# A graph network in one kernel: the second layernorm's shift made by GpSimd, and three older arrangements of layernorm work put in place of newer ones

## The chip, the cores and the metric

The kernel runs on one core of one Trainium2 chip. The metric is device time in microseconds (us) of the whole program, median of 3 runs. Engines are named as in the profile: PE is TensorE (matmuls), PEld its weight loads, DVE is VectorE, ACT is ScalarE, POOL is GpSimd, SP is SyncE (it issues transfers here). "L85" is line 85 of the kernel before.

## The reference

Four graph layers, each with a residual and a layernorm. N is 4096 nodes, D is 256 features; `adj` is a 0/1 matrix of 4096 x 4096.

```python
def _layernorm(x, axis=-1, eps=1e-5):
    m = jnp.mean(x, axis=axis, keepdims=True)
    v = jnp.var(x, axis=axis, keepdims=True)
    return (x - m) / jnp.sqrt(v + eps)

# layer 0: graph attention, 8 heads of 32 features
node_feats = (x @ W.T + b).reshape(num_nodes, num_heads, half)
attn_logits = logit_parent[:, None, :] + logit_child[None, :, :]
attn_logits = jax.nn.leaky_relu(attn_logits, 0.2)
attn_logits = jnp.where(jnp.abs(adj_matrix)[..., None] != 0.0, attn_logits, 0.0)
attn_probs = jax.nn.softmax(attn_logits, axis=1)
out = jnp.einsum('ijh,jhc->ihc', attn_probs, node_feats)
# layer 1
A = DIAG_LAMBDA * jnp.diagonal(adj) + adj
out = A @ (x @ weight) + bias
# layer 2: two steps of diffusion (R) and of attention that keeps the top 0.9 of each row (A)
for n in range(STEPS):
    A = _top_p_attention(Xa, W1, W2, W3)
    Xf = R @ Xf
    Xa = A @ Xa
    Z = Z + Xf @ U1[n].T + Xa @ U2[n].T
h = X + Z          # then a layernorm of its own with gain and offset
# layer 3
agg = adj @ x / jnp.maximum(deg, 1.0)
out = jax.nn.relu(jnp.concatenate([x, agg], axis=-1) @ W + b)
# after each layer: x = _layernorm(x + layer(x))
```

In layer 1, `jnp.diagonal(adj)` is added to every row of `adj`; so every row of the product gets the same row vector, the sum of `diag[j] * support[j]`. The kernel calls it `row` once the bias is in it.

## The kernel before

Rows are held in 32 blocks (`NB`) of 128 partitions. `X` is the state, in SBUF throughout. A layernorm takes mean and variance on VectorE, the reciprocal deviation on GpSimd (L84, L85) and the normalise (L92) on VectorE or another engine:

```python
    def moments(self, pool, src):
        ...
        for q in range(n):
            nc.vector.bn_stats(stats[:, q, :], src[:, q, :])                                   # L81
            nc.vector.bn_aggr(mv[:, q, :], stats[:, q, :])                                     # L82
        nc.gpsimd.tensor_scalar_add(var, mv[:, :, 1], EPS)                                     # L84
        nc.gpsimd.tensor_tensor(rstd, var, self.power.to_broadcast([P, n]), ALU.pow)           # L85
        return mv, rstd

    def layernorm(self, pool, dst, src, engine=None):
        mv, rstd = self.moments(pool, src)
        for q in range(src.shape[1]):
            (engine or self.nc.vector).tensor_scalar(dst[:, q, :], src[:, q, :], mv[:, q, 0:1], rstd[:, q:q + 1],
                                                     op0=ALU.subtract, op1=ALU.mult)           # L92
```

Layer 0 works through two halves (heads 0 to 3, 4 to 7), four tiles `it` of 1024 rows each, four heads each: 32 heads' turns in all. In a head's turn, for each of 8 pieces, ScalarE or VectorE makes signs (L272, L265), VectorE makes the mask `gt` of them and of the adjacency (L274, L267), and PE multiplies it (L280):

```python
            self.sums0(both, nlc, fac, lpd, nad, zd, gmd, lambda: row_logits(first, 0, 0))
            self.open_x()
            self.load1()                        # issues layer 1's weight and bias, ScalarE's queue (L111, L117)
            ...
            later = []
            per_head = Q // 2 // (H // 2)       # 1
            for half in range(2):
                for it in range(N // IT):
                    ...
                    if half:
                        ...  # X rows and y0 (what the first half stored) are loaded
                    for hh in range(H // 2):
                        h = half * (H // 2) + hh
                        lpb = row_logits(work.tile([P, IT], F32, name="lpb"), h, it) if h or it else first
                        ...
                        for g in range(NB // K):
                            gt = work.tile([P, K, IT], FP8, name="gt", bufs=4)
                            ...  # signs (L265 or L272, four each), mask (L267 or L274), 32 matmuls (L280)
                        ...  # the head's tail on VectorE, L285 to L296: y
                        for xs in later[:per_head]:
                            self.layernorm(work, xs, xs, nc.gpsimd)
                        del later[:per_head]
                    if not half:
                        ...  # y is stored
                        continue
                    engine = nc.vector if i0 + Q == NB else nc.gpsimd
                    for q in range(0, Q, 2):
                        xs = X[:, i0 + q:i0 + q + 2, :]
                        engine.tensor_add(xs[:, :, :D // 2], xs[:, :, :D // 2], y0[:, q:q + 2])     # L308
                        engine.tensor_add(xs[:, :, D // 2:], xs[:, :, D // 2:], y[:, q:q + 2])      # L309
                        if i0 + Q == NB:
                            self.layernorm(work, xs, xs)
                        else:
                            later.append(xs)
```

At its very start (`sums0`) VectorE folds the attention vectors into the weights; `self.diag` is the diagonal, loaded during that part:

```python
            for t, cs in ((w0, (0, 1)), (b0, (0,))):
                for c in cs:
                    for s in range(2):
                        prod = work.tile([P, H, C], F32, name="prod", bufs=1)
                        nc.vector.tensor_mul(prod, ...)                                             # L390
                        nc.vector.tensor_reduce(t[:, c, D + s * H:D + (s + 1) * H], prod, AX.X, ALU.add)  # L391
            ...
            nc.vector.tensor_copy(self.diagr, self.diag)                                            # L456
```

Layer 1. The adjacency pieces of a block are made one block ahead, on VectorE (L185) and ScalarE (L183) in turn, and there is room for the pieces of two blocks:

```python
            row = pool.tile([P, D], F32, name="row1")
            nc.vector.tensor_add(row, pd[:, :D], bias)
            nc.vector.tensor_add(row, row, pd[:, D:])                                               # L699
            nas = []
            ahead = self.adj_pieces(work, nas, 0)
            for b in range(NB):
                ps = psum.tile([P, 512], F32, name="ps_adj")
                now, ahead = ahead, None
                for g, a in enumerate(now):
                    nc.sync.dma_start(self.adjs[b, :, g * 8:(g + 1) * 8, :], a.bitcast(F32))        # L708
                    for k in range(8):
                        jc = g * 8 + k
                        nc.tensor.matmul(ps, a[:, k, :], XD[:, jc]..., start=(jc == 0), stop=(jc == NB - 1))  # L711
                if b + 1 < NB:
                    ahead = self.adj_pieces(work, nas, b + 1)
                xb = X[:, b:b + 1, :]
                nc.vector.tensor_add(xb[:, 0], xb[:, 0], ps[:, :D])                                 # L716
                nc.vector.tensor_add(xb[:, 0], xb[:, 0], ps[:, D:])                                 # L717
                nc.vector.tensor_add(xb[:, 0], xb[:, 0], row)                                       # L718
                self.layernorm(work, xb, xb)
```

After a block is normalised, ScalarE issues its store `xd <- X` (L807, written in layer 2). Layer 2's second step ("step 1") closes each of the 32 blocks with two layernorms in a row; the second is applied by ScalarE (`fma`, the profile's L910) as `rstd * h + shift`:

```python
                    mv, rstd = self.moments(work, h)
                    shift = small("shift")
                    nc.vector.scalar_tensor_tensor(shift, mv[:, 0, 0:1], -1.0, rstd, op0=ALU.mult, op1=ALU.mult)  # L1290
                    fma(hb, hb, rstd, shift)
```

Of the kernel before, what the change touches and what calls it, by code (L numbers as in the profile page):

```python
# [9 lines left out]
F32 = mybir.dt.float32  # L10
I32 = mybir.dt.int32
F32R = mybir.dt.float32r
# [10 lines left out]
P = 128  # L23
# [28 lines left out]
class Net:  # L52
# [9 lines left out]
    def constants(self):  # L62
        nc = self.nc
        pool = self.ctx.enter_context(self.tc.tile_pool(name="const", bufs=1))
        self.ident = pool.tile([P, P], F32, name="ident")
        make_identity(nc, self.ident)
        self.power = pool.tile([P, 1], F32, name="power")
        nc.vector.memset(self.power, -0.5)
        self.deg = pool.tile([P, self.NB], F32, name="deg")
        self.diag = pool.tile([P, self.NB], F32, name="diag")  # L70
        self.diagr = pool.tile([P, self.NB], F32R, name="diagr")

# [14 lines left out]

    def layernorm(self, pool, dst, src, engine=None):

        mv, rstd = self.moments(pool, src)  # L90
        for q in range(src.shape[1]):
            (engine or self.nc.vector).tensor_scalar(dst[:, q, :], src[:, q, :], mv[:, q, 0:1], rstd[:, q:q + 1],  # L92
                                                     op0=ALU.subtract, op1=ALU.mult)

# [99 lines left out]
    def layer0(self):  # L194
# [7 lines left out]
        with ExitStack() as ctx:  # L202
# [9 lines left out]

            def row_logits(t, h, it):
                nc.gpsimd.dma_start(t, bass.AP(tensor=lpd.tensor, offset=lpd.offset + h * N + it * IT, ap=[[0, P], [1, IT]]))
                return t

            first = pool.tile([P, IT], F32, name="lpb0")


# [14 lines left out]
            na = gp.tile([P, NB, IT], U8, name="na")  # L234

            later = []
            per_head = Q // 2 // (H // 2)
            for half in range(2):
                for it in range(N // IT):
# [10 lines left out]
                    for hh in range(H // 2):  # L250
                        h = half * (H // 2) + hh
                        lpb = row_logits(work.tile([P, IT], F32, name="lpb"), h, it) if h or it else first
                        z = work.tile([P, Q, C1], F32, name="z")
# [42 lines left out]
                        nc.vector.tensor_mul(y[:, :, hh, :], t1[:, :, :C], r.unsqueeze(2).to_broadcast([P, Q, C]))  # L296
# [7 lines left out]

                    engine = nc.vector if i0 + Q == NB else nc.gpsimd
                    for q in range(0, Q, 2):
                        xs = X[:, i0 + q:i0 + q + 2, :]
                        engine.tensor_add(xs[:, :, :D // 2], xs[:, :, :D // 2], y0[:, q:q + 2])  # L308
                        engine.tensor_add(xs[:, :, D // 2:], xs[:, :, D // 2:], y[:, q:q + 2])  # L309
# [52 lines left out]

    def sums0(self, both, nlc, fac, lpd, nad, zd, gmd, then):

# [5 lines left out]
        with ExitStack() as ctx:  # L370
# [73 lines left out]
            self.factors0(wp, ps, both, nlc, fac)  # L444
            then()

# [231 lines left out]
    def layer1(self):  # L678
        nc, tc, NB, D, X = self.nc, self.tc, self.NB, self.D, self.X
        with self.ctx1 as ctx:  # L680
            pool, w1, bias, dg = self.pool1, self.weight1, self.bias1, self.diagr
            work = ctx.enter_context(tc.tile_pool(name="l1w", bufs=2))
# [20 lines left out]
            for b in range(NB):  # L703
# [14 lines left out]
                nc.vector.tensor_add(xb[:, 0], xb[:, 0], row)  # L718
                self.layernorm(work, xb, xb)


    def layer2(self):
# [3 lines left out]
        with ExitStack() as ctx:  # L726
# [543 lines left out]
            def close(step, b, two):  # L1270
# [12 lines left out]
                else:  # L1283
# [5 lines left out]
                    shift = small("shift")  # L1289
                    nc.vector.scalar_tensor_tensor(shift, mv[:, 0, 0:1], -1.0, rstd, op0=ALU.mult, op1=ALU.mult)  # L1290
                    fma(hb, hb, rstd, shift)
# [195 lines left out]
```

## Time and profile before

| | |
|---|---|
| time, median of 3 runs | 4482.35 us (4478.71 to 4483.64) |
| span of the profiled execution | 4477.0 us |
| PE busy | 4236.7 us, 95% |
| VectorE busy | 3339.2 us, 75% |
| ScalarE busy | 2759.6 us, 62% |
| GpSimd busy | 387.2 us, 9% |

A "group" in the profile is all instructions of one line, engine and shape: its count, its busy time in us, the mean of one in ns, and the idle time of the engine just before them with what ended it. The "chain of waits" lists who waited for whom, in total us, times, and the longest. Busy time is an average over stages with different limits. Layer 0's heads run from about 616 to 1350 us in this execution, layer 1 to 1637, layer 2's second step from about 2970 to 4215, layer 3 from there.

### The profile page before, as it was taken

The numbers are of one execution on the slowest core, as the hardware profiler recorded it, in microseconds if no ns is written. First come the engines' busy times: TensorE is split into PE (matmuls) and PEld (weight loads), VectorE is DVE, ScalarE is ACT, GpSimd is POOL, SyncE is SP. The second block draws the span as 40 slices with busy tenths as digits, with TensorE's granted clock in tenths as the row PEclk, the third lists the DMA queues.
The fourth block names the chain that finished last, engine by engine and source line by source line (L and its number), as shares of the span: only waits on it lengthen the run. The fifth ranks groups of instructions, "written<-read, shape, count | busy, mean of one in ns | idle before, by whom it ended". The sixth has DMA issues, their size and how long they took to land. (4 is left out here: it accounts for less than half of the span.)

```text
span 4477.0 us, 70563 instructions
## 1 busy us (share of the span) xinstructions
PE 4236.7 (95%) x25625; PEld 3409.6 (76%) x25625; DVE 3339.2 (75%) x7641; ACT 2759.6 (62%) x5501; POOL 387.2 (9%) x554
## 2 busy tenths in 40 slices
PE   8999989999989999999999999887999999999799
PEld 6899989999987866677777777664666666666587
DVE  7632259999983448977777778398989999989254
ACT  5533369999973235766666666267667777776232
POOL 0111101113330100000000000001000000000011
PEclk9999999999999999999999999998999999999899
DMA  4765553342316953022222222530122222222541
GB/s 130 225 199 176 178 208 99 100 141 68 94 31 272 369 208 126 27 79 80 80 81 81 87 90 81 198 110 27 58 68 73 76 80 80 79 67 73 190 140 47
DMA packets 277779, 523.49 MB, mean 117 GB/s; under 512 B 36774, under 2 KB 112294, under 8 KB 273318
## 3 DMA queue, kind: packets, MB, share of 16 engines
q1 hardware_dynamic: 179268, 356.20, 23.8%
q10 hardware_dynamic: 85282, 122.62, 8.0%
q0 software_dynamic: 12864, 39.99, 2.9%
q8 instruction: 207, 3.39, 0.3%
q14 instruction: 158, 1.29, 0.1%
HBM read 363.63 MB, written 155.06 MB: 116 GB/s over the span
## 5 line engine op out<-in xcount | busy, mean ns | idle before, releaser
L1236 PE MATMUL ps_a<-X,aT 128*128 128x256 f32 x4096 | 963.9, 387 | 28.0 <-ACT aT L1233 27.3
L1236 PEld LDWEIGHTS ps_a<-X,aT 128*128 128x128 f32 x4096 | 762.9, 191 | 293.7 <-ACT aT L1233 137.6
L280 PE MATMUL acc<-gm,gt 128*128 128x198 bf16 x8192 | 704.7, 248 | 25.5 <-issue 14.7
L280 PEld LDWEIGHTS <-gt 128*128 128x128 fp8e4 x8192 | 700.8, 97 | 29.4 <-issue 14.9
L272 ACT ACTIVATE sg<-lpb,nlc 128x1024 fp8e4<-128x1024 f32 x640 | 671.3, 1135 | 59.5 <-DVE gt L274 34.6
L160 PE MATMUL ps_r<-XD,adj_piece 128*128 128x512 f32 x2048 | 510.9, 401 | 13.4 <-DMA adj_piece<-adjs 12.8
L497 PE MATMUL pz<-src,ar 128*128 128x264 f32 x4096 | 510.0, 287 | 12.8 <-DVE ar L487 10.6
L497 PEld LDWEIGHTS pz<-src,ar 128*128 128x128 f32 x4096 | 506.6, 189 | 16.1 <-DVE ar L487 13.2
L1233 ACT COPY aT<-ps_tp 128x512 f32<-128x512 f32 x512 | 277.4, 583 | 358.8 <-PE ps_tp L1231 356.9
L971 ACT ACTIVATE ja<-e,nc 128x2048 uint8<-128x2048 f32 x240 | 478.6, 1994 | 0.5 <-issue 0.2
L160 PEld LDWEIGHTS ps_r<-XD,adj_piece 128*128 128x128 f32 x2048 | 383.7, 190 | 113.3 <-DMA adj_piece<-adjs 26.8
L898 PE MATMUL ps_logit<-kT,q 64*128 64x512 f32 x1024 | 462.5, 637 | 4.0 <-ACT e L902 3.9
L917 DVE SCALAR_TENSOR_TENSOR v<-e,c 128x4096 bf16<-128x4096 f32 x100 | 447.3, 4473 | 7.3 <-ACT c L945 6.5
L1053 DVE MAX8 cand<-v 128x8 f32<-128x256 f32 x1024 | 360.6, 412 | 2.2
L1100 DVE SCALAR_TENSOR_TENSOR e<-e,edge 128x512 f32<-128x512 f32 x512 | 347.3, 746 | 1.5
L490 ACT ACTIVATE nb<-a 128x512 uint8<-128x512 f32 x256 | 156.3, 630 | 294.4 <-DMA a<-in_adjt_dram 281.8
L183 ACT ACTIVATE adj_piece<-na 128x1024 fp32r<-128x1024 fp8e4 x128 | 135.3, 1059 | 314.2 <-PE ps_adj L1393 95.3
L84 POOL TENSOR_SCALAR ln_var<-ln_mv 128x1 f32<-128x1 f32 (+1 forms) x144 | 60.4, 419 | 3040.0 <-DVE ln_mv L82 1384.2
L1231 PE MATMUL ps_tp<-ident,e 128*128 128x128 f32 x2048 | 273.1, 275 | 38.5 <-DVE e L1100 25.8
L1049 DVE SCALAR_TENSOR_TENSOR v<-e,hi 128x2048 f32<-128x2048 f32 x128 | 300.9, 2351 | 1.7
L1231 PEld LDWEIGHTS ps_tp<-ident,e 128*128 128x128 f32 x2048 | 242.0, 142 | 76.5 <-DVE e L1100 28.9
L902 ACT ACTIVATE e<-ps_logit 128x1024 f32<-128x1024 f32 x256 | 261.2, 1021 | 50.3 <-PE ps_logit L898 34.7
(304 smaller groups left out, 5353.8 us busy)
## 6 DMA issues: line engine op xcount, KB each, us to landing
adj_piece<-adjs SPq DMA_DIRECT2D x512, 256.0 KB
a<-in_adjt_dram SPq DMA_DIRECT2D x256, 256.0 KB
adjs<-adj_piece SPq DMA_DIRECT2D x128, 512.0 KB
na<-nad SPq DMA_DIRECT2D x64, 512.0 KB
na<-nad ACTq DMA_DIRECT2D x32, 1024.0 KB
nad<-nb POOLq DMA_DIRECT2D x128, 128.0 KB, 3.4
lpb<-lpd POOLq DMA_DIRECT2D x32, 512.0 KB, 4.2
xfd<-part ACTq DMA_DIRECT2D x63, 256.0 KB
```

The source lines that it names most:

```text
L160: nc.tensor.matmul(ps, a[:, k, :], rhs(jc).rearrange("p s d -> p (s d)"), start=(jc == 0 and own is None), stop=(jc == self.NB - 1))
L272: nc.scalar.activation(sg[:, k, :], lpb, AF.Sign, scale=-1.0, bias=nlc[:, jc, h:h + 1], saturate=False)
L280: nc.tensor.matmul(acc[:, q, :6 * C1], gt[:, k, q * P:(q + 1) * P], gm[:, jc, hh, :], start=(jc == 0 and q % 2 == 0), stop=(jc == NB - 1 a ...
L497: nc.tensor.matmul(pz[q][:, t, :W], ar[:, q, k, :], src[:, jc, t, s], start=(jc == 0 and s == 0), stop=(jc == NB - 1 and s == 1))
L898: nc.tensor.matmul(pl[:, s, :], q[s * A:(s + 1) * A, :], kT[s * A:(s + 1) * A, c * 512:(c + 1) * 512], start=True, stop=True)
L917: nc.vector.scalar_tensor_tensor(junk, e, c, e, op0=ALU.is_ge, op1=ALU.mult, accum_out=S)
L971: nc.scalar.activation(ja, e[:, s * HALF:(s + 1) * HALF], f, bias=nc1, accum_out=fs[:, i + s:i + s + 1])
L1049: nc.vector.scalar_tensor_tensor(v, ec, hi, ec, op0=ALU.is_lt, op1=ALU.mult, accum_out=sb[:, s:s + 1])
L1053: nc.vector.max(cand[:, 8 * j:8 * j + 8], v[:, k * 256:(k + 1) * 256])
L1100: nc.vector.scalar_tensor_tensor(ec, ec, edge[:, j:j + 1], ec, op0=ALU.is_ge, op1=ALU.mult)
L1231: nc.tensor.transpose(pt[:, k * P:(k + 1) * P], e[:, jc * P:(jc + 1) * P], self.ident)
L1236: nc.tensor.matmul(pa[:, :D], aT[:, k * P:(k + 1) * P], X[:, jc, :], start=(jc == 0), stop=(jc == NB - 1))
```

## The change

The title's part: `shift`, the product of mean, deviation and −1, is made by GpSimd right after the deviation that GpSimd has just made, so that VectorE doesn't wait for GpSimd at that place and ScalarE's `fma` depends on one engine less. In place of it the changed kernel lacks several arrangements that the kernel before has: layer 0's additions and layernorms go back to VectorE, all of a tile in one go after its last head; the first head's row of logits is no longer loaded ahead of the rest; `X += row` of layer 1 is done by GpSimd and first, not by VectorE and last; `prod` has two buffers; and the diagonal is cast in layer 1.

```diff
-    def layernorm(self, pool, dst, src, engine=None):
+    def layernorm(self, pool, dst, src):
 ...
-            self.sums0(both, nlc, fac, lpd, nad, zd, gmd, lambda: row_logits(first, 0, 0))
+            self.sums0(both, nlc, fac, lpd, nad, zd, gmd)
 ...
-            later = []
-            per_head = Q // 2 // (H // 2)
 ...
-                        lpb = row_logits(work.tile([P, IT], F32, name="lpb"), h, it) if h or it else first
+                        lpb = work.tile([P, IT], F32, name="lpb")
+                        nc.gpsimd.dma_start(lpb, bass.AP(tensor=lpd.tensor, offset=lpd.offset + h * N + it * IT,
+                                                         ap=[[0, P], [1, IT]]))
 ...
-                        for xs in later[:per_head]:
-                            self.layernorm(work, xs, xs, nc.gpsimd)
-                        del later[:per_head]
 ...
-                    engine = nc.vector if i0 + Q == NB else nc.gpsimd
                     for q in range(0, Q, 2):
                         xs = X[:, i0 + q:i0 + q + 2, :]
-                        engine.tensor_add(xs[:, :, :D // 2], xs[:, :, :D // 2], y0[:, q:q + 2])
-                        engine.tensor_add(xs[:, :, D // 2:], xs[:, :, D // 2:], y[:, q:q + 2])
-                        if i0 + Q == NB:
-                            self.layernorm(work, xs, xs)
-                        else:
-                            later.append(xs)
+                        nc.vector.tensor_add(xs[:, :, :D // 2], xs[:, :, :D // 2], y0[:, q:q + 2])
+                        nc.vector.tensor_add(xs[:, :, D // 2:], xs[:, :, D // 2:], y[:, q:q + 2])
+                        self.layernorm(work, xs, xs)
 ...
-                        prod = work.tile([P, H, C], F32, name="prod", bufs=1)
+                        prod = work.tile([P, H, C], F32, name="prod")
 ...
-            then()
 ...
-            nc.vector.tensor_copy(self.diagr, self.diag)
 ...
-            pool, w1, bias, dg = self.pool1, self.weight1, self.bias1, self.diagr
+            pool, w1, bias = self.pool1, self.weight1, self.bias1
+            dg = pool.tile([P, NB], F32R, name="dg")
+            nc.vector.tensor_copy(dg, self.diag)
 ...
                 xb = X[:, b:b + 1, :]
+                nc.gpsimd.tensor_add(xb[:, 0], xb[:, 0], row)
                 nc.vector.tensor_add(xb[:, 0], xb[:, 0], ps[:, :D])
                 nc.vector.tensor_add(xb[:, 0], xb[:, 0], ps[:, D:])
-                nc.vector.tensor_add(xb[:, 0], xb[:, 0], row)
                 self.layernorm(work, xb, xb)
 ...
-                    nc.vector.scalar_tensor_tensor(shift, mv[:, 0, 0:1], -1.0, rstd, op0=ALU.mult, op1=ALU.mult)
+                    nc.gpsimd.tensor_scalar(shift, mv[:, 0, 0:1], rstd, -1.0, op0=ALU.mult, op1=ALU.mult)
```

More of the change, by code (lines that the diff above doesn't have):

```diff
@@ L70, in constants @@
         self.diag = pool.tile([P, self.NB], F32, name="diag")
-        self.diagr = pool.tile([P, self.NB], F32R, name="diagr")
     def moments(self, pool, src):
@@ L86, in moments @@
         return mv, rstd
-    def layernorm(self, pool, dst, src, engine=None):
+    def layernorm(self, pool, dst, src):
         mv, rstd = self.moments(pool, src)
         for q in range(src.shape[1]):
-            (engine or self.nc.vector).tensor_scalar(dst[:, q, :], src[:, q, :], mv[:, q, 0:1], rstd[:, q:q + 1],
-                                                     op0=ALU.subtract, op1=ALU.mult)
+            self.nc.vector.tensor_scalar(dst[:, q, :], src[:, q, :], mv[:, q, 0:1], rstd[:, q:q + 1],
+                                         op0=ALU.subtract, op1=ALU.mult)
     def transposed(self, psum, pool, src, name, bufs=2, out=None):
@@ L211, in layer0 @@
             lpd = dram.tile([H, N], F32, name="lpd")
[L213 to L217, printed above, removed]
             nad = self.nad
@@ L361, in factors0, with sums0 @@
         nc.scalar.dma_start(self.fits, fits)
-    def sums0(self, both, nlc, fac, lpd, nad, zd, gmd, then):
+    def sums0(self, both, nlc, fac, lpd, nad, zd, gmd):
         nc, tc, NB, D, N = self.nc, self.tc, self.NB, self.D, self.N
```

## The prediction

> **What bounds the kernel now.** I read the page's busy shares first, because they say which engine can set the time at all.
>
> ```profile
> PE 4236.7 (95%) x25625; PEld 3409.6 (76%) x25625; DVE 3339.2 (75%) x7641; ACT 2759.6 (62%) x5501; POOL 387.2 (9%) x554
> ```
>
> TensorE (PE) is busy 95% of 4477 us, so anything is worth time only where it opens or closes a gap on PE. GpSimd (POOL) is idle 91% of the time and looks free. That share is an average; what counts is the waits behind GpSimd, so I read the chain of waits next.
>
> ```profile
> POOL ln_var L84 <- DVE ln_mv L82: 1384.2, 121, 65.9
> ACT adj_piece L183 <- DVE X L92: 64.3, 19, 3.4
> ACT h L910 <- DVE shift L1290: 47.6, 25, 6.6
> DVE shift L1290 <- POOL ln_rstd L85: 22.3, 32, 1.0
> PE acc L280 <- issue: 14.7, 1, 14.7
> ```
>
> The columns are: who waited for whom, total us, times, longest. The reader is to see two things. `shift` costs VectorE 22.3 us of waiting in 32 places, and ScalarE waits 47.6 us for it: that is what the title's change aims at. And in layer 1 ScalarE waits 64.3 us for the normalise L92, which itself waits for GpSimd: layer 1 has GpSimd's L84 and L85 in a loop that leads to PE. Then stage by stage, the busy time in five stretches: the head loop of layer 0, layer 1, two parts of layer 2's second half (its "step 1" in the code), and the end.
>
> ```profile
> core 0: us, PE busy (x) PEld busy (x) DVE busy (x) ACT busy (x) POOL busy (x), PEclk, DMA share, GB/s
> 616.00:1331.00 715.00, 704.28 (x8192) 700.49 (x8190) 683.38 (x876) 665.21 (x635) 158.28 (x135) 0.99 0.32 102
> 1350.00:1637.00 287.00, 278.75 (x1249) 229.53 (x1249) 136.19 (x334) 97.05 (x143) 25.20 (x64) 0.99 0.78 307
> 2970.00:3232.00 262.00, 222.94 (x954) 156.13 (x954) 239.56 (x652) 176.18 (x466) 19.55 (x24) 0.93 0.12 39
> 3232.00:4211.00 979.00, 932.94 (x4039) 661.83 (x4037) 860.84 (x2273) 653.46 (x1690) 50.15 (x100) 1.00 0.25 83
> ```
>
> The head loop is PE-bound by a hair (DVE busy 683 of 715 us); layer 1 is PE-bound with DVE half idle; step 1 is DVE-bound only in its first quarter (240 of 262 us), afterwards PE leads (933 of 979).
>
> Last, what an operation costs on GpSimd (groups by shape) and how layer 1's loop runs (timeline):
>
> ```profile
> L92 POOL TENSOR_SCALAR X<-X,ln_mv,ln_rstd 128x256 f32<-128x256 f32 x24 | 50.3, 2104 | 1.3
> L309 POOL TENSOR_TENSOR X<-X,y 128x256 f32<-128x256 f32 x12 | 15.3, 1306 | 3.3 <-DVE y L296 3.3
> L308 POOL TENSOR_TENSOR X<-X,y 128x256 f32<-128x256 f32 x12 | 14.2, 1210 | 17.5 <-DMA y<-yd 17.5
> ```
>
> ```profile
> 1407.87 0.41 DVE L699 TENSOR_TENSOR row<-row,ps_sup 128x256 f32<-128x256 f32 x1
> ...
> 1410.00 0.43 DVE L718 TENSOR_TENSOR X<-X,row 128x256 f32<-128x256 f32 x1
> ...
> 1411.93 0.23 POOL L84 TENSOR_SCALAR ln_var<-ln_mv 128x1 f32<-128x1 f32 x1 [65.90 <-DVE ln_mv L82]
> 1412.24 0.57 POOL L85 TENSOR_TENSOR ln_rstd<-ln_var,power 128x1 f32<-128x1 f32 x1
> 1412.85 0.41 DVE L92 TENSOR_SCALAR X<-X,ln_mv,ln_rstd 128x256 f32<-128x256 f32 x1 [1.16 <-POOL ln_rstd L85]
> ```
>
> `row` is complete at 1408.28, block 0's deviation at 1412.81, its normalise at 1413.26. A block of layer 1 takes PE 7.25 us (block starts 1412.52, 1419.77, 1427.03).
>
> **What the Trainium skill says.** "GPSIMD Engine Reference", § 4.1 Engine selection, puts an elementwise operation with two inputs at about 2 times VectorE's time on GpSimd. Here it is worse: 128x256 adds took 1.13 to 1.18 us back to back on GpSimd against 0.43 on VectorE (L718), 2.7 times. "SBUF — State Buffer", § Who interferes with whom: a VectorE instruction with two SBUF inputs and a GpSimd instruction that reads SBUF block each other. The trace agrees in kind: GpSimd's L92 has a mean of 2.10 us and single ones of 1.22 to 3.71, and VectorE's three masks that took 3.37 us at 730.8 beside GpSimd's adds take 2.08 alone. "TensorE: Matmul & The Clock Gate", § What's actually happening: after an idle window of about 3.4 us TensorE runs at half clock until it has been busy as long. Here, after stalls of 3.05 and 3.07 us in the head loop some 20 matmuls came 0.17 us apart in place of 0.085, about 1.7 us more; after one of 2.30 us none did. So a stall over 3 us costs 1.7 us on top.
>
> **The change part by part.** I also looked at the order in which the changed program puts its instructions into each engine's queue, which the scheduler decides and the diff doesn't show.
>
> *Start (up to 80 us).* A second `prod` buffer, and the cast of `diag` gone from VectorE's queue there (it waited 2.2 us for its load at 14.5). The last sum of w ends at 17.33 before; without that wait it is ready at about 14.5. Some of it returns, as ScalarE's transposes wait too: −2 (0.5 to 3).
>
> *Into the head loop.* Before, the first head's logits are loaded early and ScalarE signs three of the first four pieces (601.9, 603.3) before it issues layer 1's weight loads, which hold it until 612.26; the fourth comes at 613.24 and PE starts at 615.75. In the changed order both weight loads stand ahead of all 640 signs. So four signs of 1.05 us follow 613.2, not one: 3 × 1.05 = 3.1, and the first load of logits. +3.5.
>
> *Head loop, first half.* The first half's part y0 is added as soon as it has been stored and loaded again (L308, at 730, 815 and 901, among the first half's heads). Before, GpSimd adds it and VectorE's heads beside it take 22.6 to 23.1 us in place of 20.98. After, VectorE does the four adds itself (1.3 us) and, being in order, waits 1 to 2 us for the load first. Its slack is 21.76 − 20.98 = 0.78 us a head (PE's 256 matmuls of 85.0 ns against the period between L285s); the masks that PE has in hand (below) hide most. +1.5.
>
> *Head loop, second half.* Before, the adds and normalises on GpSimd slow VectorE in the heads after each of three i-tiles; PE loses 2.75, 5.3, 5.34, sum 13.4 us (heads of 24.43, 26.99, 27.02 against 21.68). After, VectorE takes each tile's whole layernorm in a burst. Its length is seen in the last i-tile, which is on VectorE in both: 1335.4 to 1346.8, 11.4 us, 3.7 of them waits for GpSimd's deviation. In the new order it stands in two lumps among the masks `gt`, which leave about 10.2 and 4.8 us between one mask and the next. A mask feeds PE for 32 × 85 ns = 2.7 us and there are four, so PE has at most three in hand, 8.2 us: 15.0 − 8.2 ≈ 7 us of stall, a little less for the first tile, where the lumps lie otherwise, a little more where fewer are in hand. I put 19 to 22 for three, with the clock's cost, against 13.4. +7.
>
> *Layer 1.* `X += row` moves from VectorE to GpSimd, and no longer waits for PE, only for `row`. The scheduler therefore runs it ahead: GpSimd's queue is 11 adds, L84 of block 0, 1 add, L85, 16 adds, L84 of block 1, 1 add, L85, 3 adds, and then L84/L85 alone. The queue is in order. At 1.14 us per add block 0's deviation is ready at 1408.3 + 12 × 1.14 + 0.23 + 0.57 ≈ 1422.9, not 1412.8. VectorE and ScalarE also run in order, behind L92 and behind the store of X that waits for it, so the adjacency pieces of block 2 come about 7 us late. Block 1's deviation: 1422.9 + 17 × 1.14 + 0.8 ≈ 1443.1; ScalarE's piece of block 3 comes then, some 14.7 us of stall on PE beyond the first. With 1.7 us twice for the clock: 7.1 + 14.7 + 3.4 = 25.2. If an add without VectorE beside it takes 0.9 us (the shortest seen is 0.91), the same sum gives 17. I take +21. Nothing of it comes back, as PE is the bound in the other 28 blocks. The last block's tail has one add of 0.43 less: −0.5.
>
> *Layer 2, step 1.* 32 shifts leave VectorE: 0.16 us each plus 22.3 us of waits, 27.4 us in all. The same product on GpSimd adds about 0.3 us (L84 took 0.22 to 0.36) after L85, and VectorE needn't wait at this place. Where VectorE is the bound, about seven blocks of 32 (2970 to 3232), the gain is 7 × 0.86 = 6; afterwards PE takes 39.3 us a block against VectorE's 38.1 and has little to win. −7, with ±10 because the scheduler re-interleaves the whole step. Layer 3 is unchanged.
>
> Sum: −2 + 3.5 + 1.5 + 7 + 21 − 0.5 − 7 = +23.5; 4482.4 + 23.5 ≈ 4506.
>
> **The rivals.** (1) The shift is worth its whole 27.4 us, as if step 1 were VectorE-bound throughout, and the rest is small: about 4455 to 4460. For it: 75% busy VectorE and ScalarE's 47.6 us of waits. Against: PE is busy 933 of 979 us after 3232. (2) GpSimd's 28 early adds in layer 1 are hidden, because something holds PE anyway or the adds are quick: about 4485. For it: GpSimd is 9% busy. Against: L92 and L183 of the next blocks stand in order behind the deviation, and the pieces are only two blocks ahead. (3) The burst in layer 0 is absorbed by the gt buffers, or the GpSimd spread was costing more than it hid: −13 in place of +7, so about 4486. Against: 8 us of lead is the most, and VectorE regains 0.78 us a head only. (4) Re-interleaving in step 1 moves it by ±10 to 30, which nothing in the profile can price.
>
> **Range and chances.** Layer 1's term may be 15 to 26, step 1's −17 to +8, the head loop's 0 to 14; in quadrature some ±14. I give 4488 to 4524. Two per cent is 90 us, which no sum of these reaches: faster 0.01, same 0.97, slower 0.02.
>
> **What would show it.** Right: layer 1 from 1350 has two PE gaps, of about 7 and 15 us, within 45 us of `row`, GpSimd's adds back to back there, and 7.25 us blocks after; PE's first head starts about 3 us later after its predecessor; three gaps of 5 to 7 us in the second half of the heads; GpSimd's L84 group without L92. In step 1 the wait for the shift moves from VectorE to ScalarE, and the stretch shrinks by well under 27 us. Wrong: layer 1 no longer than before, step 1 over 20 us shorter, or PE losing less than 13 us at the bursts.

## The result and the profile after

The changed kernel takes 4517.3 us (median of 4, 4514.0 to 4518.6), the kernel before 4481.6 us on the same chip (median of 4): ratio 1.0079, 95% interval 1.0062 to 1.0096. It is 35.7 us slower; forecast were 23.5 us, 4506 in 4488 to 4524.

In the changed kernel the line numbers are others: L84 and L85 are now L83 and L84, the normalise L92 is L91, the matmul of the heads is L272, the row's add L700, the shift L1274.

First the page's busy times of the kernel after:

```profile
PE 4249.7 (94%) x25625; PEld 3419.9 (76%) x25625; DVE 3343.3 (74%) x7625; ACT 2761.5 (61%) x5501; POOL 330.3 (7%) x570
```

No engine works more than before by more than 13 us (PE 4236.7 before), yet the span is 38 us longer: the loss is waiting. The chain of waits says for what:

```profile
POOL ln_var L83 <- DVE ln_mv L81: 1363.6, 131, 50.9
...
ACT h L894 <- POOL shift L1274: 68.0, 24, 8.7
POOL X L700 <- DVE row L683: 64.0, 1, 64.0
...
ACT adj_piece L182 <- DVE X L701: 19.4, 1, 19.4
...
PE acc L272 <- issue: 17.8, 1, 17.8
...
PE acc L272 <- DVE gt L266: 12.9, 6, 4.1
...
PE ps_adj L695 <- DVE X L702: 10.0, 1, 10.0
```

VectorE's 22.3 us of waiting for the shift are gone, as intended. But ScalarE now waits 68.0 us for it, not 47.6. The heads' first matmul waits 17.8 us, not 14.7. PE waits 12.9 us for masks in six places, and in layer 1 10.0 us in one place, where it had waited for nothing.

The same four stretches as the prediction shows, in busy time of each engine; the third and fourth again divide step 1 shortly before its seventh shift:

```profile
core 0: us, PE busy (x) PEld busy (x) DVE busy (x) ACT busy (x) POOL busy (x), PEclk, DMA share, GB/s
616.00:1347.60 731.60, 710.75 (x8192) 705.99 (x8192) 690.48 (x925) 665.33 (x636) 63.25 (x88) 0.98 0.31 99
1367.00:1667.00 300.00, 280.78 (x1249) 230.53 (x1247) 134.79 (x303) 96.96 (x143) 48.47 (x96) 0.97 0.75 294
2999.00:3276.00 277.00, 232.61 (x967) 162.59 (x968) 242.38 (x652) 178.68 (x472) 26.74 (x30) 0.91 0.12 38
3276.00:4249.00 973.00, 931.65 (x4027) 662.27 (x4025) 859.75 (x2246) 654.11 (x1686) 58.12 (x126) 0.99 0.25 83
```

The heads are 16 us longer, layer 1 13 us, and step 1's first quarter 15 us; in these PE's busy time grows by only 6, 2 and 10 us. GpSimd has 63 us in the heads where it had 158. Measured between the same instructions in both traces:

| stage | forecast | change, us |
|---|---|---|
| start, to the last matmul of layer 0's sums | −2 | −2.35 |
| from there to the heads' first matmul (15.02, 18.08) | +3.5 | +3.06 |
| heads, first half (353.20, 354.60) | +1.5 | +1.4 |
| heads, second half (361.95, 376.50) | +7 | +14.55 |
| layer 1, from the last head to its last matmul (299.0, 312.6) | +20.5 | +13.6 |
| layer 2 up to the middle of its logit matmuls, where step 1 begins | 0 | −0.9 |
| step 1 to layer 3's first matmul (1325.2, 1333.8) | −7 | +8.6 |
| layer 3 | 0 | +0.2 |
| sum | +23.5 | +38.2 |

The sum is that of two single executions (4477.0 and 4515.2); the medians differ by 35.7.

Three places carry it. The heads first: PE's timeline in the turn with the first burst.

```profile
1071.80 2.88 PE L272 MATMUL acc<-gm,gt 128*128 128x198 bf16 x32
1077.68 2.89 PE L272 MATMUL acc<-gm,gt 128*128 128x198 bf16 x32 [3.00 <-DVE gt L266]
1084.20 4.14 PE L272 MATMUL acc<-gm,gt 128*128 128x198 bf16 x24 [3.63 <-DVE gt L259]
```

A mask's 32 matmuls take 2.88 us, then PE waits 3.00, takes the next mask, and waits 3.63. The 24 after that come at half pace: 4.14 us where 32 took 2.88. In this turn and the two like it the waits from one matmul to the next sum to 7.1, 6.1 and 5.8 us, the slow matmuls after them to 2.8, 3.3 and 2.5: 27.6 us, against 13.8 before for the three turns after a tile.

Second, layer 1's timeline from `row` on:

```profile
1426.61 8.14 POOL L700 TENSOR_TENSOR X<-X,row 128x256 f32<-128x256 f32 x11 [63.95 <-DVE row L683]
...
1434.71 0.23 POOL L83 TENSOR_SCALAR ln_var<-ln_mv 128x1 f32<-128x1 f32 x1
1434.90 0.74 POOL L700 TENSOR_TENSOR X<-X,row 128x256 f32<-128x256 f32 x1
1435.60 0.57 POOL L84 TENSOR_TENSOR ln_rstd<-ln_var,power 128x1 f32<-128x1 f32 x1
1436.13 10.97 POOL L700 TENSOR_TENSOR X<-X,row 128x256 f32<-128x256 f32 x16
1436.20 11.05 DVE L91 TENSOR_SCALAR X<-X,ln_mv,ln_rstd 128x256 f32<-128x256 f32 x1 [6.21 <-POOL ln_rstd L84]
...
1447.73 1.06 ACT L182 ACTIVATE adj_piece<-na 128x1024 fp32r<-128x1024 fp8e4 x1 [19.38 <-DVE X L701]
...
1448.18 4.03 PE L695 MATMUL ps_adj<-XD,adj_piece 128*128 128x512 f32 x9 [10.05 <-DVE X L702]
```

The queue is the forecast one: 11 adds, L83, an add, L84, 16 adds. But an add takes 0.7 us here, not 1.14. And the surprise is the sixth line: one normalise of VectorE that took 0.41 us in the kernel before takes 11.05 us. It starts 0.07 us after the run of 16 adds and ends 0.15 us after it. Everything behind it on VectorE and ScalarE stands, and PE waits 10 us.

Third, step 1's first block:

```profile
3046.70 2.35 DVE L1033 SCALAR_TENSOR_TENSOR v<-e,hi 128x2048 f32<-128x2048 f32 x1
3046.77 2.42 POOL L1274 TENSOR_SCALAR shift<-ln_mv,ln_rstd 128x1 f32<-128x1 f32 x1
...
3049.22 0.60 ACT L894 ACTIVATE h<-h,shift,ln_rstd 128x256 f32<-128x256 f32 x1 [3.60 <-POOL shift L1274]
...
3050.35 1.22 PE L1220 MATMUL ps_a<-X,aT 128*128 128x256 f32 x2 [4.85 <-ACT aT L1217]
```

The shift, one element a partition, takes 2.42 us in place of 0.27, beside a VectorE instruction of 2.35 us that began 0.07 us earlier. ScalarE waits for it 3.60 us and PE behind ScalarE 4.85. Six of the 32 shifts take 1.79 to 2.42 us.

### The profile page after: what moved, and what is told of

Read it like the earlier page. It is cut to its first block, busy times and chain, and to the rows that moved or that the text cites. A ratio compares the mean times of both kernels' runs of the same rounds, so it can differ in the third digit from the quotient of the medians.

```text
span 4515.2 us, 70556 instructions
## 1 busy us (share of the span) xinstructions
PE 4249.7 (94%) x25625; PEld 3419.9 (76%) x25625; DVE 3343.3 (74%) x7625; ACT 2761.5 (61%) x5501; POOL 330.3 (7%) x570
## 5 line engine op out<-in xcount | busy, mean ns | idle before, releaser
L272 PE MATMUL acc<-gm,gt 128*128 128x198 bf16 x8192 | 710.9, 250 | 38.2 <-issue 17.8
L272 PEld LDWEIGHTS <-gt 128*128 128x128 fp8e4 x8192 | 706.0, 98 | 43.1 <-issue 18.0
L479 PEld LDWEIGHTS pz<-src,ar 128*128 128x128 f32 x4096 | 505.9, 189 | 17.1 <-DVE ar L469 14.6
L257 DVE TENSOR_SCALAR sg<-lpb,nlc 128x1024 fp8e4<-128x1024 f32 x384 | 273.6, 749 | 1.7
```

The source lines that it names most:

```text
L272: nc.tensor.matmul(acc[:, q, :6 * C1], gt[:, k, q * P:(q + 1) * P], gm[:, jc, hh, :], start=(jc == 0 and q % 2 == 0), stop=(jc == NB - 1 a ...
L479: nc.tensor.matmul(pz[q][:, t, :W], ar[:, q, k, :], src[:, jc, t, s], start=(jc == 0 and s == 0), stop=(jc == NB - 1 and s == 1))
```

## Theories

Theory A: in layer 1 and step 1 the loss comes from GpSimd and VectorE shutting each other out, and from engines that work their queues in order behind the one shut out. In layer 0 the burst on VectorE is the cause. The rivals differ by place and stand with each experiment: GpSimd's adds are simply too slow (layer 1), the title's shift is worth its 27 us and something else lost them (step 1), only the order that the scheduler picks matters, or the late row of logits and not the weight loads delays the heads. "Step 1" below is the time from the middle of the logit matmuls to layer 3's first matmul. Its four profiled executions with step 1 as in the kernel before lie between 1322.4 and 1325.2 us, and the five with step 1 as in the changed kernel between 1331.3 and 1335.8.

## Experiments

**shift_only: the title's part alone.** The kernel before with one line changed:

```diff
-  nc.vector.scalar_tensor_tensor(shift, mv[:, 0, 0:1], -1.0, rstd, op0=ALU.mult, op1=ALU.mult)
+  nc.gpsimd.tensor_scalar(shift, mv[:, 0, 0:1], rstd, -1.0, op0=ALU.mult, op1=ALU.mult)
```

> The kernel before with only the shift moved to GpSimd. Theory A (GpSimd's small operation, when it is ready, can be held up by a long VectorE instruction that VectorE now starts in place of waiting, and ScalarE then waits in order): step 1 does not get shorter, the time is 4 to 10 us longer than before, 4486 to 4491 us, and the shift takes over 1.5 us in a handful of the 32 blocks. Rival B (the title's aim): VectorE's 27 us are freed and at least the part in the VectorE-bound quarter comes back, 4474 to 4479 us (the prediction's -7), and the 8 us lost in step 1 of the changed kernel came from the other parts. Rival C (only the order of instructions matters): either sign, with all 32 shifts at about 0.27 us.

Measured: 4485.6 against 4479.5 us, ratio 1.0013 (1.0006 to 1.0021), 6.1 us slower; step 1 takes 1330.6 us, 5.4 more than before. All that came before step 1 is within 0.4 us. So the rival falls that the shift is worth its 27 us: the part for which the change was made costs time by itself. From the first shift to the eighth it loses 13.4 us, and from there to the last it gets 8.2 back. Besides six long shifts there is one long L85, in block 3 (timeline):

```profile
3119.79 4.48 DVE L917 SCALAR_TENSOR_TENSOR v<-e,c 128x4096 bf16<-128x4096 f32 x1
3119.87 4.82 POOL L85 TENSOR_TENSOR ln_rstd<-ln_var,power 128x1 f32<-128x1 f32 x1
...
3124.80 0.27 POOL L1290 TENSOR_SCALAR shift<-ln_mv,ln_rstd 128x1 f32<-128x1 f32 x1
3125.10 0.60 ACT L910 ACTIVATE h<-h,shift,ln_rstd 128x256 f32<-128x256 f32 x1 [5.21 <-POOL shift L1290]
```

In the kernel before VectorE waited at the shift and so could not begin L917 before L85 was done; L85 took 0.73 us at most. Now L917 begins 0.08 us before L85, and L85 takes 4.82. At this place the wait that the change removed had kept VectorE out of GpSimd's way. Holds as such are not new: in the kernel before six L84 of step 1 took 2.29 to 4.48 us, though no L85 and no shift was held.

**row_dve: layer 1's part undone.** The changed kernel with

```diff
-                nc.gpsimd.tensor_add(xb[:, 0], xb[:, 0], row)
                 nc.vector.tensor_add(xb[:, 0], xb[:, 0], ps[:, :D])
                 nc.vector.tensor_add(xb[:, 0], xb[:, 0], ps[:, D:])
+                nc.vector.tensor_add(xb[:, 0], xb[:, 0], row)
```

> The changed kernel with layer 1's row added by VectorE after the two PSUM adds, as before. Theory A (all that layer 1 lost comes from the adds running ahead on GpSimd): layer 1 loses its one gap of 10.4 us and the slow clock behind it, 13 to 14 us less than the changed kernel, about 4503.5 us. Rival (the later cast of the diagonal or the later start of layer 1 has part in it): only 8 to 11 us less.

Measured: 4500.4 us, ratio to before 1.0045 (1.0028 to 1.0062) where the changed kernel has 1.0079: 15 us less. Layer 1 takes 298.7 us from the last head, as before (299.0). All its loss was this one add.

**row_mid: GpSimd keeps the add, but can't run ahead.** The same three lines with GpSimd's add between VectorE's two.

> The changed kernel with GpSimd still adding the row, but in between VectorE's two PSUM adds, so that an add can't run ahead of its block. Theory A (not GpSimd's speed but its run of 16 adds back to back does the harm, because it shuts VectorE's normalise out): the gap is gone, within 2 us of the kernel with the row on VectorE, about 4504 to 4506 us, and the first normalises take 0.4 us. Rival (an add of this size on GpSimd is too slow for the chain PSUM add, row, PSUM add, moments, normalise): PE still loses time in every few blocks, no better than 4510 us.

Measured: 4503.3 us, ratio 1.0053 (1.0036 to 1.0070); layer 1 takes 298.3 us. The groups by shape in layer 1 of this kernel, where the row's add is L701 and VectorE's add ahead of it L700 (busy us, mean ns | idle before, and for whom):

```profile
L701 POOL TENSOR_TENSOR X<-X,row 128x256 f32<-128x256 f32 x32 | 24.0, 749 | 187.6 <-DVE X L700 187.6
```

```profile
L91 DVE TENSOR_SCALAR X<-X,ln_mv,ln_rstd 128x256 f32<-128x256 f32 x33 | 13.5, 413 | 25.3 <-POOL ln_rstd L84 25.3
```

The same 32 adds of 0.75 us on the same engine, and a longer chain per block, cost PE nothing. GpSimd was not too slow; its adds came too early and in a run. The rival that its adds are too slow falls.

**idle_adds: a run of adds on which nothing depends.** The kernel before, with

```diff
+            idle = work.tile([P, 2, D], F32, name="idle", bufs=1)
+            nc.gpsimd.memset(idle, 0.0)
 ...
                 xb = X[:, b:b + 1, :]
+                nc.gpsimd.tensor_add(idle[:, b % 2], idle[:, b % 2], row)
```

> The kernel before with 32 adds of the row's size on GpSimd in layer 1 that write to a tile nobody reads, two buffers of 128x256, issued once a block; VectorE keeps its own add of the row. The compiled queue of GpSimd is 16 adds, L84, 1 add, L85, 15 adds, L84, L85 alone. No instruction of another engine depends on these adds. Theory A (an instruction of VectorE[...] is shut out by a whole run of GpSimd's instructions, not by one): block 0's normalise takes about 10.4 us (15 adds at 0.69) in place of 0.41, and layer 1 takes 12 to 18 us longer. Rival (the 11 us normalise of the changed kernel was held by a dependence on the adds to X): the normalise takes 0.4 to 1.1 us; the deviations still come late, 9 us and 10 us, and layer 1 takes 10 to 15 us longer, with two gaps.

Measured, one execution: 4491.1 us; layer 1, from its first to its last matmul of the adjacency, takes 286.4 us against 271.1. PE has one gap, of 13.4 us. The timeline:

```profile
1406.51 11.09 POOL L718 TENSOR_TENSOR idle<-idle,row 128x256 f32<-128x256 f32 x15
...
1407.35 0.88 DVE L721 TENSOR_TENSOR X<-X,row 128x256 f32<-128x256 f32 x1
...
1418.98 10.23 POOL L718 TENSOR_TENSOR idle<-idle,row 128x256 f32<-128x256 f32 x15
1419.04 10.33 DVE L92 TENSOR_SCALAR X<-X,ln_mv,ln_rstd 128x256 f32<-128x256 f32 x1 [9.58 <-POOL ln_rstd L85]
...
1430.30 19.90 PE L713 MATMUL ps_adj<-XD,adj_piece 128*128 128x512 f32 x80 [13.02 <-DVE X L720]
```

L92 is held for the whole run of 15 adds that share no data with it. A dependence on their data can't be the cause. The Trainium skill, "SBUF — State Buffer", § Who interferes with whom, says that a VectorE `tensor_scalar` in a 2-port mode and a GpSimd instruction exclude each other for a whole instruction (that L92 runs in such a mode is not shown here); here it was for 15 of them, one after another, so the page's unit is too small for this case.

But a run does not always hold to its end. L721 (two SBUF inputs) ran inside the first run in 0.88 in place of 0.42 us, that is, it waited for one add at most, and L185, a `tensor_scalar` too, in 0.77 in place of 0.69. In the changed kernel the next block's normalise also began 0.07 us after a run, of three adds that took 2.62 us, and was let in after the first of them:

```profile
1450.65 0.81 DVE L91 TENSOR_SCALAR X<-X,ln_mv,ln_rstd 128x256 f32<-128x256 f32 x1 [1.34 <-POOL ln_rstd L84]
```

What decides how long an instruction is held is not shown. The page infers that a form like L721's takes only the read side of the shared port; that this is why it gets in is not shown either.

Nor does this run part the hold from the queue. Both delay block 1's work, and for the queue alone 10 to 15 us were expected as well, where 15.3 came. For the hold speak L92's own 10.33 us and the one gap where the queue alone was to give two.

**spread: layer 0's second half as before.** The changed kernel with GpSimd's adds and normalises over the next heads (`later`, `per_head`, as in the kernel before).

> The changed kernel with layer 0's second half as before: adds and normalises by GpSimd, spread over the next heads. Theory A (the burst on VectorE is what cost 14.5 us there and 1.4 in the first half): 15 to 16 us less than the changed kernel, about 4502 us, with stalls of 13 to 14 us in the heads after the tiles. Rival (the prediction's sum for this part, +7 and +1.5): 8.5 us less, about 4509 us, the rest being the later start of the heads.

Measured: 4499.5 us, ratio 1.0043 (1.0026 to 1.0059), 16 us less than the changed kernel. The heads' second half takes 364.1 us, 2.1 more than before where the changed kernel has 14.55 more; the first half 351.9, 2.7 less than in the changed kernel. Layer 1 keeps its loss (311.3 us, with a normalise of 11.05 us, the same to the hundredth, and the next one again 0.82). So the burst cost about what the table says, and the rival, my forecast of 8.5, is too small by half.

**after_l1sync and l1sync: who delays the heads' start.** Layer 1's weight and bias are loaded through SyncE's queue, from the second tile on; first in the changed kernel, then in the kernel before:

```diff
-            self.load1()
 ...
+                        if not half and it == 1 and hh == 0:
+                            self.load1()      # and load_w, load_row with queue=self.nc.sync
```

> The changed kernel with layer 1's weight and bias loaded through the queue of SyncE and later, so that they don't stand ahead of ScalarE's signs. Theory A, as predicted (the two loads hold ScalarE, three signs of 1.05 us more): the first matmul of the heads comes 3 us sooner after layer 0's sums, about 3 us less than the changed kernel. Rival (the first row of logits, which is no longer loaded ahead, lands only at about 610 us, and that holds ScalarE anyway): 1 us or less.

> The same in the kernel before, where the first row of logits is loaded ahead. Theory A: the fourth sign needn't wait until 613.2, the first matmul comes 5 to 8 us sooner; as the loads of na and gm then bound the first head, 2 to 4 us are left at its end, 4476 to 4478 us. Rival (na and gm for the first pieces are late anyway): nothing, 4479.5 us.

Measured in the changed kernel: ratio 1.0069 (1.0052 to 1.0086); the first matmul comes 16.2 us after the sums in place of 18.1. The first sign on ScalarE there still waits for the row of logits, until 10.5 us after the sums. So both are right in part: 1.9 us of the 3.1 were the weight loads, and the rest, by subtraction, I put down to the row's late landing.

In the kernel before: 4476.7 us, ratio 0.9993 (0.9986 to 1.0000). The timeline (signs L273, mask L275, matmul L281 in this kernel):

```profile
600.96 11.54 ACT L273 ACTIVATE sg<-lpb,nlc 128x1024 fp8e4<-128x1024 f32 x11 [0.28 <-issue]
...
604.22 1.23 DVE L275 SCALAR_TENSOR_TENSOR gt<-sg,na 128x1024 uint32<-128x1024 uint32 x1 [2.85 <-ACT sg L273]
605.54 4.58 PE L281 MATMUL acc<-gm,gt 128*128 128x198 bf16 x32 [6.92 <-DMA gm<-gmd]
```

ScalarE signs on without a break, and PE starts 7.2 us after the sums in place of 15.0. At the end of the first head 1.1 us of that is left and after 16 heads 2.4: the masks and matmuls of the first head then wait for the loads of `na`, the adjacency, and `gm`, what PE multiplies the masks with (6.92 us in the last line). A gain of 7.8 us at the start of a stage was worth a third of that at its end.

**shift_wait: GpSimd's shift, but VectorE waits for it.** The kernel before with the shift on GpSimd and

```diff
+                    seen = small("seen")
+                    nc.vector.tensor_copy(seen, shift)
-                    fma(hb, hb, rstd, shift)
+                    fma(hb, hb, rstd, seen)
```

> The kernel before with the shift on GpSimd, but VectorE copies it (one element a partition) and ScalarE uses the copy: VectorE waits for GpSimd as in the kernel before, so it starts no long instruction meanwhile. Theory A (the 4.9 us that step 1 loses with the shift on GpSimd alone come from GpSimd held up by VectorE's long instructions): no shift takes over 0.4 us, step 1 is within 2 us of the kernel before plus the 0.3 us that a block's chain is longer, so 4479 to 4484 us, and its first eight blocks lose at most 3 us and not 13. Theory C (the order of instructions that the scheduler chooses is what loses the time): the first eight blocks lose some other amount, 5 us or more either way, though no shift is held up.

Measured: 4482.0 against 4479.4 us, ratio 1.0004 (0.9995 to 1.0012). What the shift's line says in shift_only, here and in late_shift (below), as durations in ns, least/median/most:

```profile
L1290 POOL TENSOR_SCALAR shift<-ln_mv,ln_rstd x32: 259/266/2416, 3017.2 to 4220.0; 128x1 f32<-128x1 f32 x32
```

```profile
L1290 POOL TENSOR_SCALAR shift<-ln_mv,ln_rstd x32: 263/267/270, 3020.3 to 4223.1; 128x1 f32<-128x1 f32 x32
```

```profile
L1295 POOL TENSOR_SCALAR shift<-ln_mv,ln_rstd x24: 259/1791/2100, 3319.2 to 4231.3; 128x1 f32<-128x1 f32 x24
```

With VectorE waiting, no shift is held, no L85 either, and from the first to the eighth shift the kernel loses 0.7 us, not 13.4. That is theory A's number. But the order of instructions on VectorE and PE there is that of the kernel before too, so it doesn't part being held from order by itself. And over the whole step the profiled execution ends as far behind as shift_only's: step 1 takes 1330.6 us in both. Up to the eleventh shift, at 3405 us, 1.8 us are lost, at the sixteenth 7.0, at the last 5.2. PE's order departs from that of the kernel before at 3410.8 us and VectorE's at 3452.0 (ScalarE's already at 3116.7), so the later loss comes with a new order of instructions, and with no hold that the kernel before lacks. In the trace of shift_only the holds are seen in blocks 0 and 3; in block 2 GpSimd's L84 is held 4.48 us by L917 in both kernels, and ScalarE waits for the multiply-add 5.44 us in place of 1.49 because other work of ScalarE no longer stands ahead of it. Both causes are there, and how much each costs is not parted.

**norm_dve: no shift at all.** The kernel before with VectorE normalising in one instruction, in place of the shift and ScalarE's multiply-add:

```diff
+                    nc.vector.tensor_scalar(hb, hb, mv[:, 0, 0:1], rstd, op0=ALU.subtract, op1=ALU.mult)
```

> The kernel before with step 1's second normalise done by VectorE in one instruction (subtract the mean, multiply by the deviation), so that there is neither a shift nor ScalarE's multiply-add. The chain of a block loses 0.16 + 0.6 us and gains about 0.42. Theory A (VectorE isn't what bounds most of step 1, so what counts is ScalarE's wait in order): 0 to 6 us less than before, 4474 to 4480 us. Rival (VectorE's time counts, 0.25 us more in each of 32 blocks): up to 8 us more.

Measured: 4481.6 against 4479.4 us, ratio 1.0003 (0.9994 to 1.0012); step 1 1327.3 us. No difference that can be told from none. Neither the 0.3 us less in a block's chain nor VectorE's 8 us more is seen.

**shift_act: ScalarE makes the shift.**

```diff
-  nc.vector.scalar_tensor_tensor(shift, mv[:, 0, 0:1], -1.0, rstd, op0=ALU.mult, op1=ALU.mult)
+  less = small("less")
+  nc.scalar.mul(less, mv[:, 0, 0:1], -1.0)
+  nc.scalar.mul(shift, less, rstd)
```

> The kernel before with the shift made by ScalarE itself in two small operations (the negative mean, which it can make while GpSimd works on the deviation, and its product with the deviation). VectorE doesn't wait, as with the shift on GpSimd, but no GpSimd shift can be held up; GpSimd's L84 and L85 still can. Theory A (held shifts cause the early loss): step 1's first eight blocks lose under 4 us where the shift on GpSimd lost 13, and VectorE's freed time still gives some 5 to 8 us later: 4473 to 4478 us. Theory C (ScalarE's multiply-add stands earlier in its queue once the scheduler believes the shift to be early, and then waits for what is late in any case): the early loss stays at 8 us or more, 4480 to 4487 us.

Measured: 4510.6 us, ratio 1.0072 (1.0057 to 1.0088); step 1 1357.8 us, 32.6 more. The early part is as theory A has it: from the first shift to the eighth 2.2 us are lost, and at the twentieth the kernel is 4.0 ahead. Then it loses 36 us in twelve blocks. No theory expected that. There PE waits 1.4 to 2.8 us in every other block for ScalarE's copies of the transposed attention, but these waits sum to 11.7 us from 3719 us on, against 7.2 before from 3700 on, and don't explain the loss. No shift can be held here; one L85 is, 4.82 us in block 3, and L84, 2.29 us each in the fourteenth to eighteenth block, but that is before the loss. Where the operation sits in ScalarE's queue counts for more than what it costs; what in that order loses the time is open.

**start_l1sync: the parts that help, together.** The kernel l1sync, with the cast of the diagonal moved into layer 1, as in the changed kernel:

```diff
-            nc.vector.tensor_copy(self.diagr, self.diag)
 ...
+            dg = pool.tile([P, NB], F32R, name="dg")
+            nc.vector.tensor_copy(dg, self.diag)
```

> The kernel before with the two parts that can be taken without a loss elsewhere: layer 1's weight and bias through SyncE's queue and later, and the cast of the diagonal in layer 1, out of VectorE's queue at the start (prod keeps one buffer, since two don't fit beside the early row of logits). Expected: 2.5 us from the heads' start and 1 to 2 us from the first matmuls of layer 0, 4475 to 4477 us. Rival (layer 0's sums are bound by their loads, so the 2 us at the start don't reach the end of the sums): no better than the weight loads alone, 4476.7 us.

Measured: 4473.5 us (median of 13) against 4478.1 (of 17), ratio 0.9989 (0.9981 to 0.9997). It is the fastest here, 0.1% ahead of the kernel before and 0.9% ahead of the changed one. The last matmul of the node features, in the first stage, comes at 68.6 us in place of 71.4. Whether these 2.8 us reach the end of the sums can't be told: that point moves between 593.9 and 603.2 us from one profiled execution to the next, whatever the kernel.

**late_shift: the shift on GpSimd from the ninth block on.** The same, with

```diff
+                    if not isinstance(b, int) or b < 8:
                         nc.vector.scalar_tensor_tensor(shift, ...)
+                    else:
+                        nc.gpsimd.tensor_scalar(shift, ...)
```

> The kernel with layer 1's loads through SyncE and the diagonal's cast in layer 1 (4473.5 us, ratio 0.9989), with the shift on GpSimd as well, but only from step 1's ninth block on; the first eight stay on VectorE. If the 8 us that step 1 with all shifts on GpSimd regained after its eighth block are worth of the freed VectorE time: 3 to 8 us less, 4466 to 4470 us, ratio 0.997 to 0.998. If they were only a lag of 13 us that TensorE's lead wore off: the same as without, within 2 us, ratio 0.9985 to 0.9995. If shifts are held up in the later blocks too: slower.

Measured: 4496.1 us, ratio 1.0037 (1.0024 to 1.0051); step 1 1347.2 us, 24.8 more than without. The third expectation. The line above shows why in part: the median of its 24 shifts is 1.79 us, and 13 are over 1.7. In shift_only, with the same line of code in these blocks, four of 24 were. What is held is decided by what VectorE happens to begin just then, and a shift in the order of instructions moves it. So the 8 us that shift_only regained late can't be counted on as the worth of VectorE's freed time: with that time freed in the same blocks, this kernel loses. How much of the 24.8 is the held shifts and how much is ScalarE's order isn't parted.

## Why the prediction was right, and where it was not

The total was in the range, with the sign and two of the three large terms named. Two errors in size nearly cancelled (+7.6 and −6.9 us), which is luck, and a third term had the wrong sign.

*Start, heads' start, heads' first half.* −2, +3.5 and +1.5 were forecast, −2.35, +3.06 and +1.4 came, though the first is within that point's scatter. At the heads' start the weight loads explain 1.9 of the 3.1 (after_l1sync).

*The burst in layer 0.* The mechanism was right: two waits a tile, each for a mask, and rival 3 (absorbed by the buffers) is out. The term "19 to 22 for three, with the clock's cost" was 27.6. The waits alone sum to 19.0; the slow matmuls after them cost 8.6, where I had left 1.7 a tile in a sum that the waits already filled. The step "a stall over 3 us costs 1.7 us on top" fails in both directions: in the second turn both waits (3.86 and 2.22 us from matmul to matmul) were followed by 21 slow matmuls each, so the second needed less than 3 us, and in the first turn the wait of 3.25 us (3.00 of idle time) was followed by none. spread shows the whole term.

*Layer 1.* The order of GpSimd's queue, the running ahead and the late deviation were right, and row_dve shows that nothing else cost time there. Two steps failed. "At 1.14 us per add" was the duration in layer 0's heads; here it was 0.69 from one to the next, and the first deviation was 9.7 us after `row`, not 14.6. And "ScalarE's piece of block 3 comes then, some 14.7 us of stall on PE beyond the first" didn't happen. VectorE's first normalise was held through the run of 16 adds, so block 1's moments came only after them and found GpSimd nearly done. One gap of 10.4 us, with 1.9 us of slow matmuls in the block after it, took the place of two of 7 and 15. The queue cost the first 9.7 us, in which PE has no wait that the kernel before lacks, and the gap stands where the hold puts it. That the hold did the harm and the queue not is not shown, though: with adds of 0.69 us the forecast's own sum gives 25.2 − 29 × 0.45 ≈ 12 us without any hold, and 12.3 came. No run has the queue without the hold. What is shown is that both go with the adds that run ahead (row_dve, row_mid). For adds of 0.9 us the forecast's sum should have read 18, not 17.

*Step 1.* "Where VectorE is the bound, about seven blocks of 32, the gain is 7 × 0.86 = 6" is wrong in sign: these blocks lost 14.0 us in the changed kernel and 13.4 with the shift alone. The step took VectorE's wait as pure loss. It was also what kept VectorE from starting a long instruction while GpSimd worked. Once VectorE goes on, it begins an instruction of 2.35 or 4.48 us that reads two SBUF operands, and GpSimd's next operation lasts as long. I had cited that rule for layer 0 and not carried it here. Two readings beside it were off as well: the "three masks" of 3.37 us at 730.8 are three signs (L265), which read one SBUF tensor, and the stretch after 3232 us gives PE 37 and VectorE 34 us of busy time a block (933 and 861 us in 25 blocks), not 39.3 and 38.1. The holds are seen in the trace; that they alone make the step longer is not shown, as shift_wait ends as late without them. Rival 1, the title's aim, is out. Rival 4, re-interleaving, is real (the later loss in shift_wait, the 32.6 us in shift_act, which no hold explains, a part of the 24.8 in late_shift). The changed kernel's step 1 has the order of shift_only's on every engine; six executions with this step, in kernels that differ elsewhere, lie between 1330.6 and 1335.8 us, so the 3 us by which it was longer are within that.

## What to carry to other kernels

Work moved to an idle GpSimd must be judged by what VectorE runs beside it. A tiny operation can last as long as the VectorE instruction that has just begun (2.42 us in place of 0.27, 4.82 in place of 0.57), and a run of GpSimd's instructions can hold one VectorE instruction to its end (11.05 us in place of 0.41), though it need not. Give GpSimd's work a dependence that keeps it near its consumer (row_mid: the same adds, no loss), and before removing a wait ask which engine's work it kept undisturbed. A small edit also lets the scheduler order a whole stage anew, and that can outweigh the edit (32.6 us in shift_act), so measure it in the whole kernel.

## What was not expected of the hardware

- A VectorE `tensor_scalar` of 0.41 us took 11.05 us beside 16 GpSimd adds in a run (in three kernels: the changed one, spread and after_l1sync), and 10.33 us beside 15 that shared no data with it. The next one, which began just after a run of three adds, took 0.81 or 0.82 each time, and a two-input VectorE add inside a long run 0.88 in place of 0.42.
- GpSimd's add of 128x256 took 0.73 us in layer 1, against 1.16 to 1.18 for most in layer 0's heads, 1.6 times as long. There VectorE was at work beside it, and a partition's 256 elements lay in two pieces of 128; which of the two counts is not shown.
- Slow matmuls followed a TensorE wait of 2.22 us as well, some 4 us after the end of a longer one, where a wait of 2.30 us alone in the kernel before was followed by none, and one of 3.25 us in the changed kernel by none either.
